# Moving a mixer's step sizes, decays and first scores to earlier places in a hand-written order

## The chip, the cores and the metric

The kernel runs on one core of a Trainium2 chip. The metric is the device time in microseconds (us) of one execution. A core has five engines with a queue each: PE multiplies matrices, ACT applies activation functions, DVE and POOL do elementwise work, and SP issues the transfers here. Each engine takes the instructions of its queue in order, so an instruction that waits holds up everything queued behind it.

## The reference

Four residual blocks over 1,024 tokens (two sequences of 512) of width 512, all in float32: a block-sparse linear layer, a gated feed-forward layer (FFN), a state-space mixer, and the same FFN again. The change lies at the end of the first FFN and the start of the mixer.

```python
x = x + linear_block_sparse(layernorm(x))
x = x + ffn(layernorm(x))          # silu(x @ gate) * (x @ up) @ down
x = x + mixer(layernorm(x))
x = x + ffn(layernorm(x))

def mixer(hs):                      # H=128 heads of 64, 8 groups, chunks of 128 tokens
    proj = hs @ in_proj_w.T
    gate, hBC, dt = split(proj)     # 8192, 8192 + 2*8*128, 128 columns
    x, B, C = split(silu(conv4(hBC)))             # causal, 4 taps per channel
    dt = softplus(dt + dt_bias)                   # the step sizes
    A_dt = -exp(A_log) * dt
    A_cumsum = cumsum(A_dt)                       # within a chunk
    L = exp(segment_sum(A_dt))                    # lower triangle
    M = (C @ B.T) * L                             # the scores of one head
    Y_diag = M @ (x * dt)
    decay_states = exp(A_cumsum[-1] - A_cumsum)   # the decays
    states = (B * decay_states).T @ (x * dt), carried from chunk to chunk
    Y_off = (C @ states) * exp(A_cumsum)
    y = Y_diag + Y_off + D * x
    return (rmsnorm(y) * norm_w * silu(gate)) @ out_proj_w.T
```

## The kernel before, in words

**Order.** PE, ACT and DVE run in the order in which the program is written (a manual schedule names these three). A planner of the compiler places the instructions of POOL and SP from its own estimates. So for three engines the order of the lines below is the order of the queues, and the Python generators with their `next(...)` calls only serve to interleave several pieces of work by hand.

**Tiles.** Activations lie with channels on the 128 partitions and 512 tokens (one sequence, `b` = 0 or 1) along the free axis. `xn_t` holds the normalised, transposed input. A projection of 256 channels by 1,024 tokens is done in `seven`: seven products of 2 by 2 blocks instead of eight, in three PSUM banks x, y, z, with additions on DVE in between. Each product is two matmuls, and a float32 matmul shows as two records. The right-hand combinations `tq` are made once by `quarters` (two on DVE, one on POOL) and `last_quarter` (POOL), the left-hand ones `ws` by `left_sides` (four on POOL). The seven steps are: x, with a copy on ACT; y, then one addition on DVE; z; y again, then two additions on DVE and the first of four results; x again, second result; y, addition, third; z, addition, fourth.

**Results.** A result of `x_front` (the mixer's x) or `group` (B and C, tiles `b_t` and `c_t`) goes through `conv`: one ACT instruction, and three taps on DVE (L554) that wait in a list until `drain(n)` issues n of them. A result of `g_front` (the gate) is passed through silu on ACT. The tags `proj` and `yo` have three PSUM banks each and `tr` has two; a bank is free again after its last reader, which for `conv` is the third tap.

**Step sizes and decays.** `step_sizes` multiplies `xn_t` by the 128 columns of weights `w_dt` (tile `pd`, 16 matmuls for each sequence), adds the bias on DVE, and makes the softplus out of Abs, Exp, Ln and Exp on ACT with additions and products on DVE; `adt` is that times the negative exponential of `A_log`. All of it is done on both sequences at once, 1,024 elements wide. `decays` makes the running sums for both: `pacs` (transposed, copied to `acs_t`, one of three buffers of `room`, and stored to `acs_d` in DRAM), `pa` (copied to `acs`), `pl` (totals), then `dec` and `e_last`.

**Scores.** `half_scores(k, ...)` does the k-th of eight heads of a pair of channel tiles: for an even k it loads `bc` (the running sums of two heads, broadcast from `acs_d`); then four Relu instructions and an Exp on ACT make `m`, and another Exp makes `ce`. A product on DVE (`m` times `gm`, held back in a list until `flush`) and one on POOL (`ce` times C) follow. `m` and `ce` have five buffers each. `group_scores` transposes B and makes `gm` from B and C.

**Stages.** The mixer has 32 phases of two channel tiles. Phase 0 (before the loop) makes step sizes, x, B and C, decays and gate; phase `ph` of the loop makes the x and gate of the next two tiles while it scans (`tokens`, `both_states`, `half_scan`) the two before. In the first FFN, `for t in range(NT)` (L402) makes the down projection, tile `ffn_o`, eight tiles of 128 tokens; after each, `to_mixer` stores the tile, turns (transposes) the normalised tile of two steps before, and normalises this one.

Of the kernel before, what the change touches and what calls it, by code (L numbers as in the profile page):

```python
# [8 lines left out]
F32 = mybir.dt.float32  # L9
# [15 lines left out]
G = 8  # L25
# [12 lines left out]
def kernel(  # L38
# [280 lines left out]
    def ffn(which, first, waiting, after):  # L319


        with tc.tile_pool(name=f"ffn{which}", bufs=1) as pool:
# [79 lines left out]
            for t in range(NT):  # L402
                po = psum.tile([P, DIM], F32, tag="proj", name="ffn_o", bufs=3)
                for fc in range(NFC):
                    nc.tensor.matmul(  # L405
                        po,
                        lhsT=h_t[:, fc, t * P : (t + 1) * P],
                        rhs=down[:, fc, :],
                        start=(fc == 0),
                        stop=(fc == NFC - 1),  # L410
                    )
                nc.vector.tensor_add(x_sb[:, t, :], x_sb[:, t, :], po)  # L412
                after(t)


    def mixer(waiting):

        with ExitStack() as st:
# [13 lines left out]
            dt = sc.tile([P, NT, H], F32, name="dt")  # L432
            acs = sc.tile([P, NT, H], F32, name="acs")
# [9 lines left out]
            w_dt = weights()[:, :, 0, :]  # L443
            nc.sync.dma_start(
                w_dt, win_t[:, 2 * INTER + 2 * G * P :].rearrange("(kc p) h -> p kc h", p=P)
            )
            row = const.tile([P, 2, H], F32, name="row")
            dtb, aneg = row[:, 0, :], row[:, 1, :]
            nc.sync.dma_start(dtb, dt_bias.to_broadcast([P, H]))
            nc.sync.dma_start(aneg, a_log.to_broadcast([P, H]))  # L450
            nc.scalar.activation(aneg, aneg, AF.Exp)
            nc.vector.tensor_scalar(aneg, aneg, -1.0, None, ALU.mult)

            def step_sizes(wdt, pool):

                v = pool.tile([P, NT, H], F32, tag="bc", name="v", bufs=3)

                def pre(b):
                    pd = psum.tile([P, NCH, H], F32, tag="tr", name="pd")
                    for c in range(NCH):  # L460
                        t = b * NCH + c
                        for kc in range(KC):
                            nc.tensor.matmul(
                                pd[:, c, :],
                                lhsT=xn_t[:, kc, t * P : (t + 1) * P],
                                rhs=wdt[:, kc, :],
                                start=(kc == 0),
                                stop=(kc == KC - 1),
                            )
                    nc.vector.tensor_tensor(  # L470
                        v[:, b * NCH : (b + 1) * NCH, :],
                        pd,
                        dtb.unsqueeze(1).to_broadcast([P, NCH, H]),
                        ALU.add,
                    )

                e = pool.tile([P, NT, H], F32, tag="bc", name="e", bufs=3)
                u = pool.tile([P, NT, H], F32, tag="bc", name="u", bufs=3)  # L480
                pre(0)
                yield
                pre(1)
                nc.scalar.activation(e, v, AF.Abs)
                nc.scalar.activation(e, e, AF.Exp, scale=-1.0)
                yield
                nc.vector.tensor_scalar(u, e, 1.0, None, ALU.add)
                nc.vector.scalar_tensor_tensor(e, u, -1.0, e, ALU.add, ALU.subtract)
                nc.scalar.activation(dt, u, AF.Ln)
                nc.scalar.activation(u, dt, AF.Exp, scale=-1.0)  # L490
                yield
                nc.vector.tensor_mul(e, e, u)
                nc.vector.tensor_sub(dt, dt, e)
                nc.vector.scalar_tensor_tensor(dt, v, 0.0, dt, ALU.max, ALU.add)
                adt = pool.tile([P, NT, H], F32, tag="bc", name="adt", bufs=3)
                nc.vector.tensor_tensor(
                    adt, dt, aneg.unsqueeze(1).to_broadcast([P, NT, H]), ALU.mult
                )
                yield adt

            def decays(pool, adt):

                for b in range(2):
                    acs_t = room()
                    pt = psum.tile([H, SEQ], F32, tag="tr", name="pacs")
                    for c in range(NCH):
                        nc.tensor.matmul(
                            pt[:, c * P : (c + 1) * P],
                            lhsT=adt[:, b * NCH + c, :],
                            rhs=tri,  # L510
                            start=True,
                            stop=True,
                        )
                    nc.vector.tensor_copy(acs_t, pt)
                    nc.sync.dma_start(acs_d[:, b * SEQ : (b + 1) * SEQ], acs_t)
                for b in range(2):
                    cs = slice(b * NCH, (b + 1) * NCH)
                    pa = psum.tile([P, NCH, H], F32, tag="tr", name="pa")
                    pl = psum.tile([P, NCH, H], F32, tag="tr", name="pl")
                    nc.tensor.matmul(pa, lhsT=tri, rhs=adt[:, cs, :], start=True, stop=True)  # L520
                    nc.tensor.matmul(pl, lhsT=ones, rhs=adt[:, cs, :], start=True, stop=True)
                    nc.scalar.copy(acs[:, cs, :], pa)
                    nc.vector.tensor_tensor(
                        dec[:, b], pl[:, : NCH - 1], acs[:, b * NCH : (b + 1) * NCH - 1, :], ALU.subtract
                    )
                    nc.scalar.activation(dec[:, b], dec[:, b], AF.Exp)
                    nc.scalar.activation(e_last[:, b], pl[:, 1 : NCH - 1], AF.Exp)

            wrk = st.enter_context(tc.tile_pool(name="wrk", bufs=2))

            def load_pair(*cts):

                w = weights()
                if cts[1] == cts[0] + 1:
                    cols = slice(cts[0] * P, (cts[0] + 2) * P)
                    nc.sync.dma_start(
                        w, win_t[:, cols].rearrange("(kc p) (j c) -> p kc j c", p=P, c=P)
                    )
                else:
                    for j, ct in enumerate(cts):  # L540
                        nc.sync.dma_start(
                            w[:, :, j, :],
                            win_t[:, ct * P : (ct + 1) * P].rearrange("(kc p) c -> p kc c", p=P),
                        )
                return left_sides(w)
# [28 lines left out]

            def load_group(g):
                return load_pair(2 * NCT + g, 2 * NCT + G + g)
# [126 lines left out]
            def scores(ct, b, hh, bc, c_t, gm):  # L703

                h = 2 * ct + hh
# [12 lines left out]
                mults.append(lambda: nc.vector.tensor_mul(m, m, gm))  # L718
                ce = wrk.tile([P, NCH - 1, P], F32, name="ce", bufs=5)
                nc.scalar.activation(ce.rearrange("p c l -> p (c l)"), bc[:, hh, P:], AF.Exp)  # L720
                nc.gpsimd.tensor_mul(ce, ce, c_t[:, P:].rearrange("p (c l) -> p c l", l=P))  # L721
# [55 lines left out]
            wx = load_pair(NCT, NCT + 1)  # L777
            wbc = load_group(0)

            steps_dt = step_sizes(w_dt, wrk)  # L780
            next(steps_dt)
            while waiting:
                turn(waiting.pop(0))
            quarters()
            next(steps_dt)
            last_quarter()
            steps = x_front(0, wx, xcs)
            groups[0] = []
            steps_bc, made = group(0, wbc, "yo")
            next(steps)  # L790
# [3 lines left out]
            next(steps)  # L794
            drain(3)
            adt = next(steps_dt)
            run(steps)
            next(steps_bc)
            next(steps_bc)
            drain(3)  # L800
            next(steps_bc)
            next(steps_bc)
            drain(3)
            next(steps_bc)
            next(steps_bc)
            drain(3)
            run(steps_bc)
            wg = load_pair(0, 1)
            decays(wrk, adt)
            gate, later = g_front(wg, gts)  # L810
            next(gate)
            drain(3)
            next(gate)
            drain(3)
            next(gate)
            for u in units:
                silu(xcs[u], xcs[u])
            next(gate)
            drain()
            run(gate)  # L820
            for b in range(2):
                for x in made[b]:
                    silu(x, x)
            for dst, src in later:
                silu(dst, src)
# [5 lines left out]
            heads = {}  # L831
            def half_scores(k, c, heads):

                j, b = units[k // 2]
                if k % 2 == 0:
                    heads[j, b] = []
                    heads["bc"] = load_sums(c + j, b)
                c_t, b_tok, gm = groups[c // CTG][b]
# [269 lines left out]
```

## Time and profile before

| | us |
|---|---|
| median of three runs | 2360.16 (2359.36 to 2364.12) |
| the profiled execution | 2362.27 |
| its span, first to last instruction | 2360.6 |
| PE busy in the span | 2302.2 |
| down projection of the first FFN | 221.4 to 319.7 |
| mixer from there to the first product of its phase 2 | 319.7 to 431.1 |
| mean granted PE clock, of full | 0.992 |

Busy time of PE overlaps a little from one matmul to the next and counts a matmul at a slow clock as busy, so a share near 100% means only that PE hardly stood still. In the lists of waits the columns are the engine and line that waited, the engine, tile and line that ended the wait, the total in us, the number of waits and the longest. In the timeline they are start, length, engine, line, operation, output and inputs, shape and count, and in brackets the idle time before it with what ended it. In the table of windows each engine has its busy time, and PEclk is the clock that PE was granted.

### The profile page before, as it was taken

To read this page: it belongs to the slowest core of one execution; us is meant where nothing else is said; L and a number is where in the kernel's file an instruction comes from. 1 tells how busy PE (TensorE), PEld (TensorE's weight loads), DVE (VectorE), ACT (ScalarE), POOL (GpSimd) and SP (SyncE) were. 2 spreads that over 40 slices of the span, in tenths; PEclk is the share of its full clock that TensorE was granted. 3 is DMA by queue.
4 is the path that set the end of the run, shared out by engine and by line. 5 is a ranking of instruction groups with operands and counts; after the bars stand their busy time and mean duration, and the time that the engine had idled before them with its cause. 6 is when DMAs were issued, how large, how long until landed. Compare 5 with 4: busy or idle time off the path is not lost. (4 is left out here: it accounts for less than half of the span.)

```text
span 2360.6 us, 27338 instructions
## 1 busy us (share of the span) xinstructions
PE 2302.2 (98%) x9626; PEld 1211.0 (51%) x9626; DVE 1617.0 (68%) x2801; ACT 1133.7 (48%) x2430; POOL 994.0 (42%) x963
## 2 busy tenths in 40 slices
PE   8999998999999999999999999999999999879999
PEld 4444444555555555555555555555555555534444
DVE  6454147877778787877878887777778788745520
ACT  2111026556656565666565656556656565521100
POOL 2663023444454444444354444444444453426600
PEclk9999999999999999999999999999999999989999
DMA  5662012222221222122222222222221222236500
GB/s 183 193 203 91 18 40 90 72 72 64 79 80 60 76 79 74 63 72 81 69 66 81 72 66 79 72 72 67 77 81 61 74 80 63 90 114 216 186 14 22
DMA packets 145576, 201.39 MB, mean 85 GB/s; under 512 B 6944, under 2 KB 91808, under 8 KB 145440
## 3 DMA queue, kind: packets, MB, share of 16 engines
q1 hardware_dynamic: 145440, 199.66, 26.6%
q8 instruction: 76, 1.25, 0.2%
q14 instruction: 60, 0.49, 0.1%
HBM read 194.91 MB, written 4.72 MB: 85 GB/s over the span
## 5 line engine op out<-in xcount | busy, mean ns | idle before, releaser
L165 PE MATMUL proj<-xn_t,w 128*128 128x512 f32 x996 | 464.9, 598 | 7.6 <-ACT ce L720 7.0
L721 POOL TENSOR_TENSOR ce<-ce,c_t 128x384 f32<-128x384 f32 x256 | 269.4, 1056 | 457.5 <-ACT ce L720 456.4
L763 PE MATMUL po<-wo,gt 128*128 128x512 f32 x992 | 436.8, 595 | 0.0
L710 ACT ACTIVATE m<-bc,acs 128x128 f32<-128x128 f32 x1024 | 324.6, 389 | 10.3 <-PE py L729 10.3
L165 PE MATMUL proj<-tq,ws 128*128 128x512 f32 x664 | 308.1, 595 | 9.3 <-DVE xc L554 3.7
L763 PEld LDWEIGHTS po<-wo,gt 128*128 128x128 f32 x992 | 184.6, 190 | 219.6 <-issue 194.9
L165 PEld LDWEIGHTS proj<-xn_t,w 128*128 128x128 f32 x996 | 182.2, 191 | 206.6 <-issue 187.8
L718 DVE TENSOR_TENSOR m<-m,gm 128x512 f32<-128x512 f32 x256 | 219.9, 880 | 2.7 <-ACT m L717 2.7
L554 DVE SCALAR_TENSOR_TENSOR xc<-proj,cw,xc 128x511 f32<-128x511 f32 (+2 forms) x288 | 213.5, 742 | 2.5
L658 POOL TENSOR_TENSOR x_dec<-x_dt,dec 128x384 f32<-128x384 f32 x128 | 129.4, 1021 | 181.8 <-DVE x_dt L654 181.2
L165 PEld LDWEIGHTS proj<-tq,ws 128*128 128x128 f32 x664 | 122.1, 190 | 160.6 <-issue 142.6
L151 POOL TENSOR_TENSOR ws<-w 128x256 f32<-128x256 f32 x96 | 72.5, 755 | 307.3 <-DMA w<-in_win_t_dram 292.7
L405 PE MATMUL ffn_o<-down,h_t 128*128 128x512 f32 x448 | 193.4, 592 | 0.0
L729 PE MATMUL py<-m,x_dt 128*64 128x128 f32 x2048 | 183.4, 277 | 3.1 <-DVE m L718 3.1
L773 DVE TENSOR_TENSOR x_sb<-x_sb,po 128x512 f32<-128x512 f32 x248 | 167.8, 678 | 20.6 <-PE po L763 19.6
L756 POOL TENSOR_TENSOR sq_acc<-sq_acc,y 128x512 f32<-128x512 f32 x128 | 177.1, 1398 | 1.4 <-ACT y L755 1.4
L717 ACT ACTIVATE m<-m 128x512 f32<-128x512 f32 x256 | 161.4, 630 | 7.4
L551 ACT ACTIVATE xc<-proj,cb,cw 128x512 f32<-128x512 f32 x96 | 71.1, 775 | 177.4 <-DVE proj L194 156.5
L165 PE MATMUL proj<-tq,w 128*128 128x512 f32 x332 | 156.0, 592 | 0.0
L165 PE MATMUL proj<-xn_t,ws 128*128 128x512 f32 x332 | 156.0, 592 | 0.0
L738 PE MATMUL py<-ce,state 128*64 128x128 f32 x1536 | 151.7, 274 | 0.0
L729 PEld LDWEIGHTS py<-m,x_dt 128*64 128x64 f32 x2048 | 125.3, 138 | 31.1 <-issue 18.2
(164 smaller groups left out, 3257.8 us busy)
## 6 DMA issues: line engine op xcount, KB each, us to landing
bc<-acs_d SPq DMA_DIRECT2D x128, 512.0 KB, 3.7
w<-in_win_t_dram SPq DMA_DIRECT2D x64, 512.0 KB, 3.8
wo<-in_wo_t_dram SPq DMA_DIRECT2D x31, 512.0 KB, 3.7
wi<-in_gate_w_dram SPq DMA_DIRECT2D x14, 512.0 KB, 3.9
zi<-in_gate_z_dram SPq DMA_DIRECT2D x14, 512.0 KB, 5.1
sf<-in_gate_s_dram SPq DMA_DIRECT2D x14, 512.0 KB, 4.7
wi<-in_up_w_dram SPq DMA_DIRECT2D x14, 512.0 KB, 4.6
zi<-in_up_z_dram SPq DMA_DIRECT2D x14, 512.0 KB, 5.7
```

Source lines behind the costliest of these rows:

```text
L165: nc.tensor.matmul(ps, lhsT=a[:, kc, :], rhs=b[:, kc, :], start=(start and kc == 0), stop=(stop and kc == KH - 1), skip_group_check=True,)
L405: nc.tensor.matmul(po, lhsT=h_t[:, fc, t * P : (t + 1) * P], rhs=down[:, fc, :], start=(fc == 0), stop=(fc == NFC - 1),)
L554: nc.vector.scalar_tensor_tensor(dst[:, s:], ps[:, : SEQ - s], cw[:, t, 3 - s : 4 - s], dst[:, s:], ALU.mult, ALU.add)
L710: nc.scalar.activation(m[:, c, :], bc[:, hh, c * P : (c + 1) * P], AF.Relu, bias=acs[:, t, h : h + 1], scale=-1.0,)
L717: nc.scalar.activation(m, m, AF.Exp, scale=-1.0)
L718: mults.append(lambda: nc.vector.tensor_mul(m, m, gm))
L721: nc.gpsimd.tensor_mul(ce, ce, c_t[:, P:].rearrange("p (c l) -> p c l", l=P))
L729: nc.tensor.matmul(py[hh * HD : (hh + 1) * HD, c * P : (c + 1) * P], lhsT=x_dt[:, c, hh, :], rhs=m[:, c, :], start=True, stop=(c == 0),)
L738: nc.tensor.matmul(py[hh * HD : (hh + 1) * HD, c * P : (c + 1) * P], lhsT=state[:, c - 1, hh, :], rhs=ce[:, c - 1, :], start=False, stop=True,
L756: nc.gpsimd.tensor_add(sq_acc[:, b, :], sq_acc[:, b, :], y)
L763: nc.tensor.matmul(po, lhsT=gts[j, b][:, c * P : (c + 1) * P], rhs=wo[:, j, :], start=(j == 0), stop=(j == PP - 1),)
L773: nc.vector.tensor_add(acc[:, t, :], acc[:, t, :], po)
```

## The change

It does four things.

1. `load_pair`, `load_group`, the step sizes and the tiles `dt` and `acs` move out of `mixer`, so that `to_mixer` can use them. The weights of the step sizes are loaded after the first tile of the down projection, those of the first x and of the first group after the second and third.
2. `step_sizes` works on one sequence. For sequence 0 it runs in the last three steps of the down projection, in scratch tiles of the FFN; for sequence 1 it runs after the first two steps of `x_front`, in the `y` tiles.
3. `decays(b)` works on one sequence. It copies `pacs` on ACT instead of DVE and takes its banks `pa` and `pl` from the tag `yo`. `decays(0)` comes after the first product of the first `x_front`, `decays(1)` after its last.
4. The scores of the first four heads come between the steps of the first group and the first gate, their POOL products later (list `ces`). The group's silus and `group_scores` move into the first gate. In phase 1 the steps of the gate, each behind up to three taps, take the place of what was run in one piece after the loop over k.

```diff
@@ ffn: after(t, sg_tile) instead of after(t)
@@ step_sizes(b, wdt, dtb, aneg, rooms): one sequence, b
+        pd = psum.tile([P, NCH, H], F32, tag="tr", name="pd")
...
+        nc.vector.tensor_tensor(v, pd, dtb.unsqueeze(1).to_broadcast([P, NCH, H]), ALU.add)
+        nc.scalar.activation(e, v, AF.Abs)
+        nc.scalar.activation(e, e, AF.Exp, scale=-1.0)
+        yield
+        nc.vector.tensor_scalar(u, e, 1.0, None, ALU.add)
+        nc.vector.scalar_tensor_tensor(e, u, -1.0, e, ALU.add, ALU.subtract)
+        nc.scalar.activation(d, u, AF.Ln)
+        nc.scalar.activation(u, d, AF.Exp, scale=-1.0)
+        yield
+        nc.vector.tensor_mul(e, e, u)
+        nc.vector.tensor_sub(d, d, e)
+        nc.vector.scalar_tensor_tensor(d, v, 0.0, d, ALU.max, ALU.add)
+        nc.vector.tensor_tensor(acs[:, cs], d, aneg.unsqueeze(1).to_broadcast([P, NCH, H]), ALU.mult)
+        yield
@@ decays(b)
+                acs_t = room()
+                pt = psum.tile([H, SEQ], F32, tag="tr", name="pacs")
...
+                nc.scalar.copy(acs_t, pt)
+                nc.sync.dma_start(acs_d[:, b * SEQ : (b + 1) * SEQ], acs_t)
+                pa = psum.tile([P, NCH, H], F32, tag="yo", name="pa", bufs=3)
+                pl = psum.tile([P, NCH, H], F32, tag="yo", name="pl", bufs=3)
...
+                nc.scalar.copy(acs[:, cs, :], pa)
                 nc.vector.tensor_tensor(
+                    dec[:, b], pl[:, : NCH - 1], acs[:, b * NCH : (b + 1) * NCH - 1, :], ALU.subtract
                 )
+                nc.scalar.activation(e_last[:, b], pl[:, 1 : NCH - 1], AF.Exp)
+                nc.scalar.activation(dec[:, b], dec[:, b], AF.Exp)
@@ mixer, phase 0: the whole of it after the change
+            wx, wbc = loaded
+            wg = load_pair(0, 1)
+            steps = x_front(0, wx, xcs)
+            turn(waiting.pop(0))
+            next(steps)
+            turn(waiting.pop(0))
             quarters()
+            steps_dt = step_sizes(1, *step_args, [y_room() for _ in range(3)])
             next(steps_dt)
             last_quarter()
+            decays(0)
             next(steps)
             next(steps_dt)
             next(steps)
             next(steps)
+            next(steps_dt)
             drain(3)
+            next(steps)
+            next(steps)
             run(steps)
+            decays(1)
+            groups[0] = []
+            steps_bc, made = group(0, wbc, "yo")
             next(steps_bc)
             drain(3)
             next(steps_bc)
+            drain(3)
             next(steps_bc)
             drain(3)
             next(steps_bc)
+            ces = []
+            half_scores(0, 0, heads, ces)
             next(steps_bc)
+            half_scores(1, 0, heads, ces)
             run(steps_bc)
             gate, later = g_front(wg, gts)
             next(gate)
             drain(3)
+            half_scores(2, 0, heads, ces)
+            next(gate)
+            drain(3)
+            half_scores(3, 0, heads, ces)
             next(gate)
             drain(3)
             next(gate)
+            drain()
             for u in units:
                 silu(xcs[u], xcs[u])
             for b in range(2):
                 for x in made[b]:
                     silu(x, x)
+            next(gate)
+            group_scores(made, groups[0], [0])
+            next(gate)
+            group_scores(made, groups[0], [1])
+            made = None
+            for f in ces:
+                f()
+            run(gate)
             for dst, src in later:
                 silu(dst, src)
@@ phase 1 (last is False): between replaces outs, and the gate starts before the loop
+                if not last:
+                    gate, later = g_front(wg, gts_new)
+                def between(k):
+                    if not last:
+                        drain(3)
+                        next(gate, None)
+                    elif front:
+                        outs(k)
                 for k in range(4):
+                    between(2 * k)
                     flush()
                     back_scores(4 + k)
...
+                    between(2 * k + 1)
...
-                if ph == 1:
-                    next(gate)
-                    next(gate)
-                    next(gate)
                 scans = half_scan(units[2:])
@@ to_mixer(t, sg_tile)
+            if t == 0:
+                state["args"] = step_weights()
+            if t in (1, 2):
+                state[t] = load_pair(NCT, NCT + 1) if t == 1 else load_group(0)
             if len(waiting_m) == 2:
                 turn(waiting_m.pop(0))
             waiting_m.append(norm_all(t))
+            if t == NCH + 1:
+                rooms = [sg_tile(*jb) for jb in ((0, 0), (0, 1), (1, 0))]
+                state["steps"] = step_sizes(0, *state["args"], rooms)
+            if t > NCH:
+                next(state["steps"])
```

## The prediction

> **What bounds the kernel now.** The page first: PE is busy for nearly the whole span, so only time in which PE stands still, or runs at a slow clock, can be won.
>
> ```profile
> PE 2302.2 (98%) x9626; PEld 1211.0 (51%) x9626; DVE 1617.0 (68%) x2801; ACT 1133.7 (48%) x2430; POOL 994.0 (42%) x963
> ```
>
> The change touches the stretch from 319.7 us (end of the down projection) to 431.1 (the first product of phase 2's x). The list of PE's waits in it adds up to 17 us:
>
> ```profile
> PE proj L165 <- ACT ce L720: 7.0, 1, 7.0
> PE yo L165 <- DVE tmp L180: 4.0, 1, 4.0
> PE proj L165 <- DVE xc L554: 1.9, 1, 1.9
> PE x_tr L650 <- ACT b_tok L595: 1.3, 1, 1.3
> ```
>
> Next PE's timeline at the two long waits:
>
> ```profile
> 350.13 5.30 PE L165 MATMUL yo<-xn_t,w 128*128 128x512 f32 x8 [3.98 <-DVE tmp L180]
> 355.27 1.88 PE L165 MATMUL yo<-tq,w 128*128 128x512 f32 x4
> ...
> 410.53 3.75 PE L165 MATMUL proj<-xn_t,w 128*128 128x512 f32 x4 [7.05 <-ACT ce L720]
> 414.07 2.26 PE L165 MATMUL proj<-tq,ws 128*128 128x512 f32 x4
> ```
>
> Four records (one product of `seven`) take 1.72 us start to start elsewhere; here they take 3.54, and eight take 5.14 instead of 3.43. So each long wait costs 1.7 to 1.8 us more in slow clock. The windows say the same (PEclk is the third figure from the end):
>
> ```profile
> 410.00:412.00 2.00, 1.47 (x2) 0.84 (x3) 2.00 (x4) 1.97 (x7) 1.00 (x1) 0.50 0.43 144
> 412.00:414.00 2.00, 2.00 (x3) 0.62 (x2) 1.96 (x3) 1.54 (x4) 1.42 (x2) 0.50 0.18 19
> ```
>
> With its slow starts, small gaps and a slack `pst`, the stretch of 111.4 us loses about 24: PE's work in it, each kind at its start-to-start time, is five times `seven` (12.02 each, 60.1), `pd` 7.2, seven groups of transposes 3.0, decays 5.2, group scores 2.4, `pst` 2.7, scans 6.0, `x_tr` of phase 2 0.9, in all 87.5. The change can't win more than 24 us.
>
> What ends the wait of 7.05 is read from DVE's timeline, since ACT's `ce` has no part in the bank that the product fills:
>
> ```profile
> 404.75 0.74 DVE L748 SCALAR_TENSOR_TENSOR y<-xc,dsk,py 128x512 f32<-128x512 f32 x1
> ...
> 407.64 1.53 DVE L554 SCALAR_TENSOR_TENSOR xc<-proj,cw,xc 128x511 f32<-128x511 f32 x2
> 409.09 0.68 DVE L718 TENSOR_TENSOR m<-m,gm 128x512 f32<-128x512 f32 x1
> 409.69 1.40 DVE L554 SCALAR_TENSOR_TENSOR xc<-proj,cw,xc 128x509 f32<-128x509 f32 x2
> ```
>
> The third tap of L554, near 410.4, frees the first bank of `proj`: DVE is the limit behind PE. Last, ACT after the scan:
>
> ```profile
> 421.63 1.28 ACT L710 ACTIVATE m<-bc,acs 128x128 f32<-128x128 f32 x4 [4.48 <-PE py L729]
> 422.94 0.63 ACT L717 ACTIVATE m<-m 128x512 f32<-128x512 f32 x1
> 423.48 0.51 ACT L720 ACTIVATE ce<-bc 128x384 f32<-128x384 f32 x1
> 424.00 1.28 ACT L569 ACT_TABLE_LOAD   x1
> 425.30 2.19 ACT L569 ACTIVATE xc<-xc 128x512 f32<-128x512 f32 x4
> 427.39 0.61 ACT L569 ACTIVATE gt<-gt 128x512 f32<-128x512 f32 x1
> 427.91 0.57 ACT L569 ACTIVATE gt<-proj 128x512 f32<-128x512 f32 x1
> ```
>
> The sixth `m` of the stage needs one of five buffers and waits for a scan; from there ACT needs 6.9 us until the first gate bank is free. PE has 6.9 us of gate products left at that time, which cover it.
>
> **What the Trainium skill says.** "TensorE: Matmul & The Clock Gate", Part 1: after an idle window of about 3.4 us PE falls to half clock, and needs about 3.4 us of work to come back. The trace agrees on the half clock (0.50) and on the way back (3.5 us), but gaps of 2.92 (at 2035.6) and 2.38 us (2087.1) were also followed by half speed, and 1.85 was not; I take 2 to 3 us as the limit. "ScalarE: Activation LUTs", What ACT_TABLE_LOAD costs: 1.28 us and a drain of 1.38. The trace has 1.28 and the next instruction 0.02 us after, no drain. Table sets: Abs is in every set, and one set has Exp and Ln. In the trace Exp after Ln loads again (335.66, 1.28 us), so I count a load each way; whether Abs needs one no run shows.
>
> **Part by part.** Work on PE is the same in all: nothing is added or removed there.
>
> *Down projection.* `pd` of sequence 0 (32 records, 3.58 us) moves ahead of the seventh tile; the mixer starts 3.58 later and has 3.58 less to do. Its ACT and DVE work for half the width (5 us with loads) and the weights' Exp lie under tiles of 12 us each; nothing after a tile waits for it but the next norm, due 12 us later. Cost 0. The last norm is different: its Sqrt needs a table load, queued behind the transpose's copy, and PE waits 1.1 us for the last transpose. If the load waits for its operand it is 1.8; if there is none, 0.5. On SP and POOL the moved loads and `left_sides` bring nothing: `w` is issued at 207.9 and 219.9 and POOL is done at 226.9 already.
>
> *Start of the mixer* (PE times of the changed kernel; the last tile ends at 323.3). x to 325.9, last transpose 327.0, `pd` to 331.0. DVE is behind: step sizes 0 (3.05), `tq` (2.5), bias at 332.5 to 333.2. ACT then needs Abs 0.55, load 1.28, Exp 0.55, two copies 1.06: `dec(0)` on DVE waits for the second, and the addition behind it, 337.4 to 338.1, holds PE's fourth step: 1.0 lost. ACT: Ln and Exp with two loads (3.7 us) end at 341.6; DVE's four products (3.05), three taps (2.24) and two additions to 348.3; ACT copies for `decays(1)` to 350.3. The bank of `pa` is free only then: 1.0 lost, and 0.25 at the addition.
>
> *First group.* DVE does taps, an addition, two more triples, then the two additions of the fourth step: 0.55 + 2.24 + 0.65 + 4.5 + 1.4, to 359.6. Step 6 waits for it: 1.6 lost. The gate's first addition waits for a copy queued behind four `conv` and two scores: 0.85 lost. ACT now runs without a break: four `conv` 2.9, four scores of 2.24 (four Relu, Exp, Exp), copy 0.55, load 1.28, four silus 2.1, `b_t`'s 0.6 = 16.4, to 376. PE has finished the gate's fifth step at 371.8 and needs that `b_t`: 4.2 lost, and 1.7 slow clock. Sum so far: 1.1 + 1.0 + 1.25 + 1.6 + 0.85 + 5.9 = 11.7; before lost 10.3 up to the same point (0.4, 4.0, 1.7, 1.5 in decays, 0.6, 1.8, 0.3 of `pst`).
>
> *Phase 1.* Scores are done, so DVE has less in front and reaches the states with PE. After the scan (403.1) it still has states and y until 404.7, and taps 2.24: PE's gate waits 4.0 (7.05 before) and pays 1.7 for the clock. But now the gate's three banks come one by one: the third waits for the addition after the second product and a triple of taps: 3.2 lost, 1.7 clock. ACT's scores 4 to 7 stand behind the gate's copy (410.7 instead of 403.4), 9.0 us; m of the seventh head lets the last scan wait 0.7. Then the chain of 6.9 us after that scan runs with no gate products left: PE has 2.4 us of scan and transposes, so 2.0 + 1.75 are lost. Sum 15.1, against 13.6 before (7.05 + 1.8 + 0.4 + 1.9 + 0.2, and 2.3 in small gaps).
>
> Sum: 26.8 against 23.9, +2.9 us. From phase 2 on the order is the same and PE hides the rest, so the shift stays. The profiled execution goes from 2362.3 to about 2365.2; the median of the runs is 2.1 lower than that execution, so 2360.2 goes to 2363.0. Unknown: each of three slow starts, 0 to 1.7, since a gap of 3.2 lies near the limit (I take all three); the load ahead of Abs, 0 or 1.28; Sqrt's, −0.6 to +0.7; DVE beside POOL, 0.68 or 0.88 for a product of two SBUF tiles, 8 of them: up to 1.6. Ends about −4 and +6.
>
> **Rivals.** *Faster, by packing.* If Abs causes the load while ACT waits (−1.3) and the row of 16.4 us starts 3 us sooner, since taps and additions overlap more than I let them, `b_t`'s wait and slow start go (−5.9), and the gate's gaps stay under the limit (−3.4): 2.9 − 9.3 = −6.4 with the 1.3 inside the first term, 2353.8. For it: before, each wait was one of few. Against it: DVE and ACT stay in written order, and every term has its row.
>
> *Slower, by the broadcast loads.* SP is in order, and the planner places it. If the first `bc` is queued behind the load of phase 1's gate weights, it waits until the group has released its buffer, 362; with 3.7 us to land (median) that is 365.7 instead of the 359.6 when ACT wants it. ACT's row, `b_t` and PE move by 6: 2369. It decides from the point when `bc` lands after 359.6. For: before, that weight load (357.6) was issued ahead of `bc` (363.5). Against: the sums are stored 12 us earlier (349.7 instead of 361.4).
>
> *It doesn't do what it says*: moving the weight loads changes nothing, since they are early already; that part is in the sum at 0.
>
> **Numbers.** A measurement of this kernel can tell about 0.2% (4.7 us) from no change. My own case (within −4 to +6, mostly no measurable change) 0.62, packing 0.17, broadcast and similar queueing 0.21. A part of my case passes 4.7 as well: faster 0.17, same 0.47, slower 0.36. Predicted 2363; its own range 2356 to 2366, with the rivals 2352 to 2370.
>
> **What would show it.** Right: PE idles about 4 us ahead of `b_tr`, with ACT solid from the first `conv` of the group to `b_t`'s silu; gate products in phase 1 wait for taps twice, at PEclk 0.5; the first x product of phase 2 comes at 434 (431 before). Wrong: no gap at `b_tr`, that product before 428; or ACT's first Relu waiting for a DMA.

## The result, and the profile after

No difference that can be told: the changed kernel's median over 14 runs is 2362.66 us (2360.05 to 2367.86). That of the kernel before, over 14 runs that include the three shown above, is 2362.95 (2359.36 to 2364.91). The ratio is 1.0003, 95% interval 0.9994 to 1.0011, that is −1.4 to +2.6 us. The first three runs of the kernel before (median 2360.16) lay at the low end of its spread, so a forecast set on them came near the number that was measured by luck: the forecast difference of +2.9 lies just outside the interval.

The profiled execution of the changed kernel took 2367.33 us (span 2365.6), at the top of its spread. What follows is therefore read beside a second profile of the same kernel, "once more", with a span of 2361.5. First the page's totals:

```profile
PE 2305.5 (97%) x9626; PEld 1212.1 (51%) x9626; DVE 1619.1 (68%) x2805; ACT 1142.4 (48%) x2442; POOL 994.7 (42%) x963
```

PE's instructions are the same in number. Its 3.3 us of extra busy time fit the slow clock that is counted further down (7.7 us in this profile, 3.9 before). Next the list of PE's waits of the changed kernel from 319 to 445 us (engine, line, engine that released it; us in all, times, longest), to be laid beside the one of before with its 7.0, 4.0, 1.9 and 1.3:

```profile
PE proj L165 <- issue: 4.1, 1, 4.1
PE b_tr L581 <- ACT b_t L559: 4.1, 1, 4.1
PE proj L165 <- DVE xc L544: 3.2, 1, 3.2
PE x_tr L637 <- ACT xc L559: 2.1, 1, 2.1
PE yo L165 <- DVE tmp L185: 1.3, 1, 1.3
PE ln_tr L128 <- DVE tmp L115: 1.0, 1, 1.0
```

Two long waits, 7.0 and 4.0, have become four of 2.1 to 4.1. The row with "issue" is phase 1's first gate product; DVE's first three taps there end near 407.4, just ahead of it. PE's timeline of the changed kernel shows what each wait cost in clock (start, duration, and in brackets the idle time before the group):

```profile
375.43 0.86 PE L581 MATMUL b_tr<-ident,b_t 128*128 128x128 f32 x3 [4.08 <-ACT b_t L559]
376.09 1.94 PE L588 MATMUL pgm<-c_t,b_t 128*128 128x128 f32 x8
377.82 2.43 PE L165 MATMUL proj<-tq,w 128*128 128x512 f32 x4
...
407.55 3.75 PE L165 MATMUL proj<-xn_t,w 128*128 128x512 f32 x4 [4.15 <-issue]
411.09 2.86 PE L165 MATMUL proj<-tq,ws 128*128 128x512 f32 x4
417.12 3.75 PE L165 MATMUL proj<-tq,ws 128*128 128x512 f32 x4 [3.17 <-DVE xc L544]
420.67 4.91 PE L165 MATMUL proj<-xn_t,w 128*128 128x512 f32 x8
...
434.85 1.18 PE L637 MATMUL x_tr<-ident,xc 128*128 128x128 f32 x8 [2.11 <-ACT xc L559]
435.86 1.88 PE L165 MATMUL proj<-xn_t,w 128*128 128x512 f32 x4
```

The records of 3.75 where 1.88 is usual are the half clock. It stands behind each of the three waits over 3 us, and the rows behind (2.43, 2.86, and 4.91 for 3.60) are still partly slow. From start to start, against the same records at full clock, the three slow starts cost 1.7, 2.8 and 3.1 us. The first x product of phase 2 comes at 435.86 here and at 432.62 in the second profile; the forecast was 434.

ACT's timeline shows why `b_tr` waits:

```profile
359.09 0.81 ACT L541 ACTIVATE c_t<-tmp,cb,cw 128x512 f32<-128x512 f32 x1 [7.31 <-DVE tmp L186]
359.81 1.26 ACT L699 ACTIVATE m<-bc,acs 128x128 f32<-128x128 f32 x4
...
371.37 1.28 ACT L559 ACT_TABLE_LOAD   x1
372.67 2.19 ACT L559 ACTIVATE xc<-xc 128x512 f32<-128x512 f32 x4
374.76 0.61 ACT L559 ACTIVATE b_t<-b_t 128x512 f32<-128x512 f32 x1
...
413.11 1.28 ACT L706 ACT_TABLE_LOAD   x1
...
430.50 1.28 ACT L699 ACTIVATE m<-bc,acs 128x128 f32<-128x128 f32 x4 [5.04 <-PE py L726]
```

From the first `conv` of `c_t` to `b_t`'s silu at 374.8 ACT has no gap: the row of work that the prediction named, 16.3 us long where 16.4 was forecast. The last row is the sixth `m`, which waits for a scan.

"Stretch" is used below for the time from the down projection's last transposes to phase 2's first x product. It is 107.8 us before (without the `pd` of sequence 0, 3.58, which the change takes out of it), 112.5 in the first profile of the changed kernel and 108.9 in the second. The rest, up to the start of the last gate product of the second FFN, is 1678.3 before, and 1678.6 and 1677.7 after: the forecast that nothing else moves holds.

### The profile page after: what moved, and what is told of

Its sections match the earlier page's. It is cut to its first block, busy times and chain, and to the rows that moved or that the text cites. A ratio compares the mean times of both kernels' runs of the same rounds, so it can differ in the third digit from the quotient of the medians.

```text
span 2365.6 us, 27346 instructions
## 1 busy us (share of the span) xinstructions
PE 2305.5 (97%) x9626; PEld 1212.1 (51%) x9626; DVE 1619.1 (68%) x2805; ACT 1142.4 (48%) x2442; POOL 994.7 (42%) x963
## 3 DMA queue, kind: packets, MB, share of 16 engines
q1 hardware_dynamic: 145440, 199.66, 26.8%
```

## The experiments

The theory: the step sizes gain, and moving scores and gate ahead turns the gain into waits for ACT's and DVE's queues, each with a slow start where it is long. The rivals: the waits stay wherever the scores are (amount of work, not order); the slow starts are an accident of one execution; the step sizes bring nothing. All ratios are to the kernel before. Runs with a ratio interval wider than ±0.1% had five runs.

**1. The changed kernel once more**, without an edit.

> The changed kernel itself once more, beside the others of this call. Theory (three slow starts that come or stay away from execution to execution): the same waits of PE at the same places in its profile, the wait ahead of b_tr again 4.1 and the one for the third bank 3.2, but less slow clock behind at least one of them, and times spread over 5 us or more. Rival (the spread comes from elsewhere, the transfers at the start for one): the slow products stand at all three places again, 3.5 us for four records.

Median 2362.05 us (2360.24 to 2366.57), ratio 0.9998 (0.9990 to 1.0006). PE's timeline of this profile:

```profile
375.71 0.90 PE L581 MATMUL b_tr<-ident,b_t 128*128 128x128 f32 x3 [4.08 <-ACT b_t L559]
...
378.12 3.36 PE L165 MATMUL proj<-tq,w 128*128 128x512 f32 x4
...
408.44 3.63 PE L165 MATMUL proj<-xn_t,w 128*128 128x512 f32 x4 [4.36 <-issue]
...
416.95 1.96 PE L165 MATMUL proj<-tq,ws 128*128 128x512 f32 x4 [3.17 <-DVE xc L544]
418.74 3.60 PE L165 MATMUL proj<-xn_t,w 128*128 128x512 f32 x8
```

The same wait, 3.17 to the hundredth, and this time no slow clock behind it: 1.96 and 3.60 instead of 3.75 and 4.91. The windows say the same (length, busy PE, PEld, DVE, ACT, POOL, SP, then PEclk, DMA share, GB/s), first profile first:

```profile
416.00:420.00 4.00, 2.88 (x4) 1.36 (x5) 1.54 (x3) 3.94 (x12) 1.52 (x2) 0.56 0.29 82
```

```profile
416.00:420.00 4.00, 3.05 (x7) 1.44 (x8) 1.80 (x3) 3.94 (x12) 1.99 (x2) 1.00 0.09 35
```

PEclk 0.56 in one, 1.00 in the other. In the profiles of the experiments below the same wait of 3.17 stands three more times, and the products behind it lost 3.1 us (late scores), 1.5 us (experiment 5) and none (experiment 4). So whether slow clock follows a pause of this length, and for how long, is a draw, and some of the kernel's spread may be that draw. The two longer waits (4.1 and 4.4) were slow both times, but not equally: the slow start at `b_tr` cost 1.7 us in the first profile and 2.7 in the second (3.36 where 2.43 stood), the one at the first bank 2.8 and 1.7. In all, the first profile lost 7.7 us in slow clock and the second 4.5.

**2. Late scores, late gate, both.** Three kernels undo parts of the fourth item: the scores of heads 2 and 3 back to phase 1; phase 1's gate back behind the loop over k; both.

```diff
@@ late scores
-            half_scores(2, 0, heads, ces)
...
-            half_scores(3, 0, heads, ces)
...
-                if last:
-                    back_scores(2)
+                back_scores(2)
...
-                if last:
-                    back_scores(3)
+                back_scores(3)
@@ late gate
-                if not last:
-                    gate, later = g_front(wg, gts_new)
...
-                    if not last:
-                        drain(3)
-                        next(gate, None)
-                    elif front:
+                    if front:
                         outs(k)
...
-                    if last:
-                        drain(1 if k < 3 else 0)
+                    drain(1 if k < 3 else 0)
...
-                if front and last:
+                if front:
                     gate, later = g_front(wg, gts_new)
+                if ph == 1:
+                    next(gate)
+                    next(gate)
+                    next(gate)
...
-                    if last:
-                        next(gate)
+                    next(gate)
```

> Edit to the changed kernel: scores 2 and 3 go back to phase 1 (between its x products, as before the change), so that ACT reaches the group's silus 4.5 us sooner. Theory A (time given back at named places): the 4.1 us wait of PE for b_t's silu ahead of b_tr and the slow clock behind it (1.7) go, less up to 1 for the last tap; phase 1 is not held up, since ACT idled there from 386 to 411. Phase 2's first x product near 431 instead of 435.9, time 4 to 5.5 us under the changed kernel, ratio to before near 0.998. Theory B (the stretch is bound by the sum of ACT and DVE work, and an order only moves the wait): the wait turns up in phase 1, and time stays within 1.5 us of the changed kernel.

> Edit to the changed kernel: in phase 1 the gate runs after the loop over k again and in the order of before, three products ahead of the second scan and four beside the next scores. Theory A: the wait of 3.2 us for the third bank with its slow clock, ACT's late scores and the uncovered 2.1 us ahead of x_tr go; one wait of about 6 to 7 us at the gate's first product stays. Phase 2's first x product near 431 instead of 435.9, 4 to 5 us less. b_tr still waits 4.1. Theory B: within 1.5 us of the changed kernel.

> Both edits together (scores 2 and 3 in phase 1, gate after the loop), which leaves the step sizes in the down projection, decays by sequence and two heads' scores in the group. Theory A: the two gains add, 8 to 10 us under the changed kernel, ratio near 0.996, phase 2's first x product near 427. Theory B: within 2 us of the changed kernel.

Measured: late scores 2362.14 (2359.39 to 2364.65), ratio 0.9995 (0.9986 to 1.0003); late gate 2358.70 (2357.02 to 2360.49), 0.9982 (0.9974 to 0.9990); both 2355.07 (2354.44 to 2355.46), 0.9966 (0.9953 to 0.9978). PE's timeline with late scores:

```profile
372.93 1.16 PE L588 MATMUL pgm<-c_t,b_t 128*128 128x128 f32 x8 [1.14 <-ACT c_t L559]
...
405.16 3.75 PE L165 MATMUL proj<-xn_t,w 128*128 128x512 f32 x4 [5.27 <-issue]
...
414.58 3.75 PE L165 MATMUL proj<-tq,ws 128*128 128x512 f32 x4 [3.17 <-DVE xc L544]
```

The 4.1 at `b_tr` is gone, with its slow start; three waits of 1.14, 0.66 and 0.34 are left of it. With the 1.7 of that slow start in the first profile it is some 3.7 us less. But DVE has the products of these two heads in front of phase 1's taps (1.92 us at 390.22) and reaches them only 2.4 us sooner (402.75 for 405.14): the wait for the first bank grows from 4.15 to 5.27, and the third bank's 3.17 and `x_tr`'s 2.1 stay. The stretch, 109.7, is 2.8 us shorter than in the first profile of the changed kernel, which had slow starts of the same size at the two banks, and 0.8 longer than in the second, which had none at the third. The expectation of −4 to −5.5 is missed: 2.1 us of waits stay in the group where it allowed 1, and 1.1 is handed back at the first bank. The medians, with both kernels spread over 5 us and more, show no gain that can be told.

PE's waits with the late gate, and then with both:

```profile
PE proj L165 <- ACT m L699: 5.3, 1, 5.3
PE b_tr L581 <- ACT b_t L559: 4.1, 1, 4.1
...
PE proj L165 <- DVE xc L544: 1.2, 1, 1.2
```

```profile
PE proj L165 <- ACT ce L709: 5.7, 1, 5.7
PE proj L165 <- DVE xc L544: 1.4, 1, 1.4
```

With the late gate the third bank's wait is 1.2 instead of 3.2 and `x_tr` doesn't wait at all, since four gate products again stand between the scan and the transposes. Against the two medians of the changed kernel that is 3.4 to 4.0 us less, a little under the 4 to 5 expected. Both together are 7.0 to 7.6 below the changed kernel and 8 below the kernel before, where 8 to 10 below the changed kernel was expected. That is more than the two gains measured alone: late scores are worth 3.6 us beside the late gate, and nothing that can be told beside the early one.

**3. Pauses filled.** Products whose result nobody reads are put into the three long waits, so that PE doesn't stop.

```diff
+            def filler(n):
+                pf = psum.tile([P, SEQ], F32, tag="tr", name="filler")
+                for i in range(n):
+                    nc.tensor.matmul(pf, lhsT=ident, rhs=xn_t[:, 0, :SEQ], start=(i == 0), stop=(i == n - 1))
...
             next(gate)
+            filler(4)
             group_scores(made, groups[0], [0])
...
                         drain(3)
+                        if k in (0, 2):
+                            filler(4 if k == 0 else 3)
                         next(gate, None)
```

> Edit to the changed kernel: matmuls whose result nothing reads are added on PE in its three long waits, 4 (3.4 us) ahead of b_tr, 4 ahead of phase 1's first gate product and 3 (2.6 us) ahead of its third. Nothing is taken away. Theory A: each wait is followed by about 3.5 us at half clock because PE stood still; with PE busy it keeps the clock, each place gains up to 1.7 us, 4 to 5 us under the changed kernel although there is more work. Rival: the slow records come from what the products wait for and not from the clock, or the added work pushes the real one; then 0 to 2 us longer.

Median of 21 runs 2360.55 (2359.67 to 2363.20), ratio 0.9991 (0.9984 to 0.9997). PE's timeline ahead of `b_tr`:

```profile
369.67 3.60 PE L790 MATMUL filler<-xn_t,ident 128*128 128x512 f32 x8
373.92 0.55 PE L581 MATMUL b_tr<-ident,b_t 128*128 128x128 f32 x3 [0.65 <-ACT b_t L559]
```

`b_tr` now takes 0.55 instead of 0.86, and no product behind a filler is slow. The gain is 1.5 to 2.1 us against the two medians of the changed kernel, less than half of the 4 to 5 that was expected, although the profiles of the changed kernel lost 7.7 and 4.5 us in slow clock. In the profile the stretch is 106.1, 2.9 and 6.4 us less than in the two of the changed kernel. That the medians show less may be because not every execution has these slow starts; it isn't settled. The spread of the runs is narrower than the changed kernel's (3.5 us over 21 runs against 7.8 over 14 and 6.3 over 13), which fits a spread that comes from slow starts.

**4. The last three gate products behind the second scan**, to cover `x_tr`'s wait.

```diff
-                        next(gate, None)
+                        if k < 4:
+                            next(gate)
```

> Edit to the changed kernel: only the first four products of phase 1's gate stay in the loop over k, the last three run behind the second scan. Theory A: the wait of 2.1 us ahead of phase 2's x_tr is there because no product of the gate is left beside ACT's 6.9 us after the scan; with 5.2 us of products there it goes, phase 2's first x product comes 2 to 3 us sooner, and the waits for the first and third bank stay as they were. Rival: the scan that now comes 5 us sooner waits for its m (ACT and DVE are late), and the time is the same within 1 us.

Median 2361.36 (2360.29 to 2363.98), ratio 0.9996 (0.9988 to 1.0004). From PE's waits:

```profile
PE py L726 <- DVE m L707: 2.0, 2, 1.7
```

And from DVE's timeline:

```profile
421.41 0.69 DVE L185 TENSOR_TENSOR gt<-gt,proj 128x512 f32<-128x512 f32 x1 [2.82 <-PE proj L165]
422.13 0.69 DVE L186 TENSOR_TENSOR gt<-gt,proj 128x512 f32<-128x512 f32 x1
422.74 2.70 DVE L707 TENSOR_TENSOR m<-m,gm 128x512 f32<-128x512 f32 x3
```

The 2.1 at `x_tr` is gone, and the scan, which now comes sooner, waits 2.0 for DVE's products instead. The time is the same, as the rival had it, but not because DVE and ACT had too much work: ACT had the first two of these three `m` ready at 418.8 and 421.0, and DVE stood idle for 2.82 us. Its additions for the gate are written ahead of these products and wait for PE. So the place in DVE's queue has a part in the scan's wait; how large a part was not tried.

**5. The step sizes of sequence 0 in the mixer**, just ahead of those of sequence 1.

```diff
+            run(step_sizes(0, *step_args, [y_room() for _ in range(3)]))
             steps_dt = step_sizes(1, *step_args, [y_room() for _ in range(3)])
...
-            if t == NCH + 1:
-                rooms = [sg_tile(*jb) for jb in ((0, 0), (0, 1), (1, 0))]
-                state["steps"] = step_sizes(0, *state["args"], rooms)
-            if t > NCH:
-                next(state["steps"])
```

> Edit to the changed kernel: the step sizes of sequence 0 run in the mixer, whole, ahead of those of sequence 1, and not in the down projection. Theory A (the start of the mixer is a chain of DVE and ACT with no room in it): that puts about 11 us of it (five activations, three loads, seven DVE instructions) into that chain and takes 3 us of DVE out; PE waits at the first running sums, and everything up to b_t's silu comes later; 5 to 8 us longer than the changed kernel. Rival (PE's order hides it): within 1.5 us.

Median 2372.29 (2370.60 to 2373.36), ratio 1.0039 (1.0026 to 1.0051): 10 us slower than the changed kernel, more than the 5 to 8 that was expected. One new row in PE's waits carries it:

```profile
PE pacs L515 <- DVE acs L480: 9.2, 1, 9.2
```

The later waits are as they were (4.1, 4.2, 3.2, 2.1), so nothing further on gives this back. The wait has a slow start too (1.8), and some 1.6 us of small waits around it go. Under the down projection the same chain of ACT and DVE costs PE at most the 0.7 by which the last transpose waits longer there (1.0 for 0.3). The kernel before did this work for both sequences at once, so the 10 us aren't what the step sizes alone gain over it.

**6. What is left on both edits.** The following kernels start from "both" of experiment 2. One puts the filler of experiment 3 ahead of phase 1's first gate product (`filler(6)`). One moves the scores of heads 0 and 1 to phase 1 as well. One runs the six taps of phase 1's x ahead of the states of the second scan. The last is that one, and in the first group the third triple of taps moves behind the additions of the fourth step.

```diff
@@ filler
                 if ph == 1:
+                    filler(6)
                     next(gate)
@@ no early scores
-            half_scores(0, 0, heads, ces)
...
-            half_scores(1, 0, heads, ces)
...
+                if ph == 1:
+                    back_scores(0)
                 flush()
                 next(steps)
+                if ph == 1:
+                    back_scores(1)
@@ taps first
                 run(steps)
+                if ph == 1:
+                    drain(6)
                 both_states(1)
@@ taps first, and the group's
             next(steps_bc)
-            drain(3)
             next(steps_bc)
+            drain(3)
             ces = []
```

> Edit to the kernel with both edits (scores 2 and 3 in phase 1, gate after the loop): six matmuls that nothing reads (5.15 us on PE) are added in its one long wait, ahead of phase 1's first gate product (5.7 us). Theory: the clock holds, the 3.5 us at half speed behind that wait go, and the time falls by up to 1.7 us to about 2353.5, unless DVE's taps hold the third bank anyhow (the second wait, 1.4 us, grows): then by 0 to 0.5. Rival: the added work costs its own length where it runs over the wait, 0 to 1 longer.

> Edit to the kernel with both edits: scores 0 and 1 go to phase 1 as well, so of the change only the step sizes in the down projection, the decays by sequence and the group scores inside the gate are left. If the early scores are worth something by themselves, this is 2 us or more longer than the kernel with both edits (phase 1's DVE and ACT have two more heads in front of the taps, so the wait for the gate's first bank grows from 5.7 to 7, as before the change). If they are worth nothing, it is within 1 us, and the whole gain is that of the step sizes and the order around them.

> Edit to the kernel with both edits: in phase 1 six taps are issued ahead of the last two states instead of behind the scan's results. Theory (the long wait of PE there is the place of the taps in DVE's order and not DVE's amount of work): the first two banks are free at the scan's end, the wait of 5.7 us goes, the third bank is free 3 us sooner, and a wait of 5 to 6 us with slow clock comes there: 2 to 3.4 us less than the kernel with both edits. Rival (amount of work): the scan then waits for m as long, within 1 us.

> Edit to the kernel of the edit before (six taps early): in the first group the third triple of taps comes behind the two additions of the fourth step and not ahead of them. Theory: PE's wait of 1.3 us for these additions goes, all that follows comes 1.3 us sooner unless the waits at pgm (1.1, for c_t's taps) take it back: 0.3 to 1.5 us less than that kernel. With all edits the ratio to before is near 0.995.

*Filler.* 2356.97 (2355.72 to 2358.63), ratio 0.9975 (0.9966 to 0.9985). PE's timeline:

```profile
406.34 1.96 PE L165 MATMUL proj<-tq,ws 128*128 128x512 f32 x4 [1.00 <-DVE xc L544]
411.05 3.28 PE L165 MATMUL proj<-tq,ws 128*128 128x512 f32 x4 [2.75 <-DVE xc L544]
```

That is 1.9 us more than "both", where 0 to 1 more was the worst expected. The second product is at full clock and ends sooner, but the next waits for the same taps, 2.75 instead of 1.43, and slow clock follows that wait. Counted from the stretch's start the third product begins at the same moment as without the filler (89.8 us), but takes 3.28 instead of 1.96. The slow start that the filler avoids ended while PE would have waited for DVE anyway, and cost nothing; the one that it brings stands where nothing covers it.

*No early scores.* 2357.75 (2356.22 to 2358.87), ratio 0.9978 (0.9970 to 0.9986), 2.7 us more than "both". PE's timeline:

```profile
406.71 3.75 PE L165 MATMUL proj<-xn_t,w 128*128 128x512 f32 x4 [7.05 <-ACT ce L709]
```

The 7.05 of the kernel before is back to the hundredth: it came from the scores that stand ahead of phase 1's taps on DVE. Two heads' scores ahead of time take 1.3 of it away; the other two (experiment 2) take another 1.1 with the early gate and 0.4 with the late one, and cost 3.7 or more at `b_tr`.

*Taps first.* 2355.53 (2353.94 to 2356.06), ratio 0.9969 (0.9956 to 0.9981): as "both". PE's timeline, and DVE's row between the second and third bank:

```profile
399.29 1.95 PE L165 MATMUL proj<-xn_t,w 128*128 128x512 f32 x4 [0.20 <-issue]
401.56 1.96 PE L165 MATMUL proj<-tq,ws 128*128 128x512 f32 x4 [0.32 <-DVE xc L544]
409.33 3.75 PE L165 MATMUL proj<-tq,ws 128*128 128x512 f32 x4 [5.82 <-DVE xc L544]
413.01 1.12 PE L726 MATMUL py<-m,x_dt 128*64 128x128 f32 x8
```

```profile
409.11 4.17 DVE L707 TENSOR_TENSOR m<-m,gm 128x512 f32<-128x512 f32 x3
```

The first wait is down to 0.20, and the third bank's has become 5.82, both as the theory had it. Its product starts 3.1 us sooner. But with "both" the slow start stood at the first bank, covered by DVE; here it stands behind the last wait, and the product and the scan take 3.1 us longer than at full clock (the scan's rows 1.12 and 0.64 for 0.66 and 0.39). In the profile that is the whole gain. The rival, a scan that waits for DVE's products, isn't seen: PE's list has no such wait, though three of them take 4.17 in one row.

*And the group's taps.* 2350.93 (2350.17 to 2352.19), ratio 0.9952 (0.9939 to 0.9966). It is the best of all, some 12 us below both kernels. PE's timeline:

```profile
367.39 0.49 PE L581 MATMUL b_tr<-ident,b_t 128*128 128x128 f32 x3
...
406.23 3.53 PE L165 MATMUL proj<-tq,ws 128*128 128x512 f32 x4 [5.82 <-DVE xc L544]
...
420.74 1.88 PE L165 MATMUL proj<-xn_t,w 128*128 128x512 f32 x4
```

The waits of 1.3 (`yo`) and 0.40 (`gt`) are gone, and `b_tr` stands 2.24 us nearer to the stretch's start, which is what a triple of taps takes. The stretch is 98.9 against 102.5; the other 1.4 of that are less slow clock behind the third bank (`py` at 0.66 and 0.39 a row where taps first had 1.12 and 0.64), a draw. The medians differ by 4.6, of five runs each; expected were 0.3 to 1.5. Here moving taps helps, because DVE has room later in the group: it had been PE that waited for an addition queued behind six taps.

## Why the prediction was right or wrong

The chief case, mostly no measurable change, came true, and the places it named are where PE waits. Its +2.9 us is not confirmed: the two sets of runs give +0.7 and −0.5 by their ratios. The time that PE loses in the stretch shows why. Its own work there is 87.5 less 3.58, 83.9 us. "Waits" are the idle times of 0.2 us and more in PE's timeline, "slow clock" is what the products behind a pause take beyond the same records at full clock, and the rest is small gaps.

| us | before | forecast | first profile | second profile |
|---|---|---|---|---|
| waits | 17.0 | 21.7 | 17.5 | 17.5 |
| slow clock | 3.9 | 5.1 | 7.7 | 4.5 |
| small gaps | 3.0 | none counted | 3.4 | 3.0 |
| lost in all | 23.9 | 26.8 | 28.6 | 25.0 |

So the waits changed places and kept their sum. That 26.8 lies between the two profiles is partly luck: the forecast waits were 4.2 us too long, and the small gaps, of which its sum for the kernel before has 2.6 (2.3, and 0.3 of `pst`), were put at nothing for the changed kernel, without a reason. By its steps:

- *Down projection at no cost, last transpose 1.1*: 1.00, as forecast. Against running the same step sizes one after the other in the mixer, the cover is worth 10 us (experiment 5).
- *Start of the mixer.* The wait at the fourth step, forecast 1.0, was 0.33; that for `pa`'s bank, 1.0, was 0.63; the addition's 0.25 was 0. The chain of DVE and ACT was right and a little long: DVE reached the bias at 332.1 instead of 332.5, and ACT's copy for `decays(1)` ended at 349.9 instead of 350.3. Abs needed no load of its own: it runs at 332.86, and the load of 1.28 stands behind it, at 333.51, for the Exp.
- *First group.* Step 6: forecast 1.6, measured 1.32. The gate's first addition: 0.85, measured 0.40. `b_tr`: 4.2, measured 4.08, in both profiles. Its slow start: 1.7, measured 1.7 in the first profile (from this `b_tr` to the next one, 375.43 to 380.09, 4.66, where the same records take 2.94 start to start at full clock) and 2.7 in the second (375.71 to 381.31).
- *Phase 1.* First bank: forecast 4.0, measured 4.15 and 4.36. Third bank: 3.2, measured 3.17 twice. The mechanism, one bank after another behind an addition and a triple of taps, is right.
- *The three slow starts* were mis-sized. They were taken at 1.7 each, with 0 to 1.7 as the range; measured are 1.7, 2.8 and 3.1 in the first profile and 2.7, 1.7 and 0 in the second. The size came from the kernel before, where only the first four records behind the wait of 7.05 were counted; the four behind them, 2.26 for 1.88, were partly slow too, and that start cost 2.2. The Trainium skill's idle window of about 3.4 us ("TensorE: Matmul & The Clock Gate", Part 1) fits the 3.17 that went both ways, but it isn't a sharp limit: 2.75 in experiment 6 was followed by a product of 3.28. Nor does the page's way back of about 3.4 us of work hold for every start: a loss of 3.1 at half clock is a way back of some 6.3 us, an estimate that fits the windows of the first profile, where PEclk is 0.50 from 418 to 422 and 0.68 in the two us behind.
- *The end of phase 1.* The `m` of the last scan, forecast 0.7: 0 and 0.9. `x_tr`, 2.0: 2.11 and 1.3. The further 1.75 for x behind the gate bank's silu failed as a step: the product starts at 435.86, ahead of that silu, at 436.78 on ACT. The prediction took the banks strictly in turn.
- *Not foreseen*: a table load in phase 1. It lies ahead of the first Exp after silus, 1.28 us at 413.11, but the sixth `m` waits for the scan afterwards (the 5.04 at 430.50), so it cost nothing that shows.
- *The rivals.* Packing didn't happen: the gap at `b_tr` was there. Nor did the broadcast loads queue; SP's timeline:

```profile
337.98 0.37 SPq L609 DMA_DIRECT2D bc<-acs_d  x1
...
351.46 0.87 SPq L609 DMA_DIRECT2D bc<-acs_d  x2
360.44 0.37 SPq L420 DMA_DIRECT2D w<-in_win_t_dram  x1
```

The broadcasts are issued ahead of the gate's weights, and ACT's first Relu (359.81) follows `conv` without a wait. That the early weight loads change nothing is right: they are issued at 195.94, 207.95 and 220.00, as before.

So the large change moves little because its parts cancel: it shortens or takes away the waits of 4.0 and 7.05 and brings others (`b_tr`, the third bank, `x_tr`), and all of PE's waits in the stretch are 17.0 us before and 17.5 after. Laid one on the other, by ratios to the kernel before: all of the change but early scores and the early gate, 0.9978 (−5 us); with the scores of two heads, 0.9966 (−8); with those of four and phase 1's gate between the taps, 1.0003 and 0.9998 (back to nothing). What the first 5 us come from, the step sizes, the decays by sequence or the group's scores inside the gate, was not separated.

## What to carry to other kernels

A chain of small ACT and DVE work ahead of PE pays where it is put beneath a stage that PE bounds. Work moved ahead pays only while the in-order queue that it joins has room before the instruction for which PE waits next: read that queue's timeline, not the busy share. A pause of PE has two prices, the pause and a draw on the slow clock behind it, and filling it gains only where the product after it doesn't wait for another engine again. A slow start costs nothing where such a wait follows it anyway, and all of its length behind the last wait.

## What the runs showed of the hardware

- Whether slow clock follows a short pause of PE is a draw. The wait of 3.17 us stands in five profiles (two of the changed kernel, late scores, experiments 4 and 5) and was followed by slow clock in three. A wait of 2.11 at `x_tr` was followed by it once (experiment 5, PEclk 0.75 and 0.70) and not in two other profiles. Behind every wait of 3.9 us and more in the stretch it came.
- A slow start cost 1.5 to 3.1 us, also behind the same wait in the same kernel.
- DVE's product of two SBUF tiles, 0.68 us alone, took 1.39 (three in 4.17), in a row beside which POOL was adding squares of y and making `ce`. Whether POOL is the cause was not tried by itself.
